# Routed adapters taken a whole layer of a pair at a time, and one rotation of eight PSUM banks, in a four-layer conditional residual kernel

## The chip, the core and the metric

The kernel runs on one core of one Trainium2 chip. The metric is the device time of one execution in microseconds (us); smaller is better. A core has a matrix engine (PE), which reads a stationary and a moving operand from the on-chip memory SBUF and writes sums into PSUM, two engines for elementwise work (DVE and ACT), a third that here does the convolution's additions and the gathers (POOL), and a queue engine (SP) that issues most of the transfers from device memory.

## What is computed

`x` has 32 batch rows of 64 x 1024 numbers. Four residual layers follow each other; `itok_...` are integers for each row.

```python
x = x + L0(x, ..., length=itok_B_78_3631)      # a long convolution along the 1024 axis, masked by length
x = x + einsum('bsi,boi->bso', x, W1[itok_B_0_15])   # one of 16 matrices of 1024 x 1024 for each row
x = x + einsum('bij,bkj->bik', x, W2[itok_B_1_14])   # the same with a second set
x = x + L3(x, ..., lora_indices=itok_B_2_6)    # gate, up and down projections (1024 to 2752 to 1024)
                                               # with a rank-16 correction chosen for each row
```

All of it is in 32-bit floats. The second and third layers are called adapters here: each batch row needs its own 4 MB matrix, used for only 64 rows of `x`.

## The kernel before

**Chunks.** The 32 batch rows are cut into four chunks of eight (`NCK`, `BC`). The convolution is done first for all chunks. Then the adapters of chunk 0 run alone. After that, `ffn(c, ...)` (line 446) runs the fourth layer of chunk c, and between its steps it does the adapters of chunk c+1. Chunk 3 has nothing to mix in.

**An adapter.** `adapter(w, layer, b0, pending)` (line 159) takes one of the two layers for a pair of batch rows. Its loop over eight blocks `kt` of the contracted axis loads two tiles of 512 KB, one for each row of the pair (lines 184 to 187), and issues four matmuls of 64 columns by 512 (line 191). They add into two PSUM banks `acc`. Two ACT copies take the banks to `y` (line 201). `residual` (line 206) transposes `y` back through eight PE transposes into two banks `py` and adds them to `x` on DVE (line 214); it runs inside the adapter that follows. A chunk has four pairs and two layers, so eight adapters, and `adapters` (line 216) chains them.

**Pieces.** `adapter` is a generator. Before, it yields after the fourth `kt` and at its end, so each adapter is two pieces with eight tiles each, and a chunk has `NPIECE` = 16 pieces. The closure `other` (line 453) adds up shares of the fourth layer's steps: 4 for each gated step (line 464) and 5 for each down step (line 556), 113 in a chunk. It takes the next piece whenever `due[1] * 113 < due[0]`, where `due[0]` grows by the share times `NPIECE + 1`. The last piece of the chain is the residual of the last adapter.

**The fourth layer's steps.** `gated` (line 369) goes over 11 blocks `m` of the hidden axis, and for each over two halves g (gate and up). Such a step loads two 512 KB tiles `wf` (line 381), makes three combinations of them on DVE (`stationary`, lines 356 to 359: sums `s1`, `s2`, `s4`, and one difference that overwrites a tile), and issues seven products of four matmuls (lines 386 and 399 to 412). The first product reads a loaded tile as it is; the second reads `s2`, so it needs both tiles and two DVE operations. Three banks `pf` take the products. Ahead of each `m`, `expand` (line 320) puts the low-rank correction into four banks `pe`, which ACT copies to `lt` (line 338). The down projection (line 493 on) loads two tiles `wd` for each segment of three blocks and uses four banks `po` for each of four `h`.

**Buffers.** The tiles `wa`, `wf` and `wd` share one rotation of nine buffers (`wpool`, tag `w`): the load of a tile is issued on SP only when the tile nine places earlier has been read for the last time. PSUM has eight banks. Before, six of them rotate under the tag `ps` (`ps_tile`), and two under the tag `acc` (`acc_tile`), which only adapters use.

**Order.** PE's order is that of the program text (`manual_schedule`). The other engines' queues, SP's too, are ordered by a scheduler when the program is built, and each queue is then executed in order.

Of the kernel before, what the change touches and what calls it, by code (L numbers as in the profile page):

```python
# [8 lines left out]
F32 = mybir.dt.float32  # L9
# [7 lines left out]
P = 128  # L17
# [4 lines left out]
BC = B // NCK  # L22
# [9 lines left out]
KH = KT // 2  # L32
R = 16
NE = 16
NPIECE = 2 * BC
AT_GATED, AT_DOWN = 4, 5
GROUPS = (8, 8, 16, 16, 16)
HG = max(GROUPS)
# [25 lines left out]
def kernel(  # L64
# [24 lines left out]
    xpool = ctx.enter_context(tc.tile_pool(name="xpool", bufs=2))  # L89
    wpool = ctx.enter_context(tc.tile_pool(name="wpool", bufs=9))  # L90
    psum = ctx.enter_context(
        tc.tile_pool(name="psum", bufs=6, space=bass.MemoryType.PSUM)
    )

    dpool = ctx.enter_context(
# [2 lines left out]

    def ps_tile(name):
        return psum.tile([P, 512], F32, tag="ps", name=name)  # L100


    def acc_tile(name):
        return psum.tile([P, 512], F32, tag="acc", name=name, bufs=2)

    cst = cpool.tile([P, CO_N], F32, tag="cst", name="cst")
    ident = cst[:, CO_ID : CO_ID + P]
# [51 lines left out]
    def adapter(w, layer, b0, pending):  # L159
        c, lo = b0 // BC, (b0 % BC) * H  # L160
        es = []
        for b in (b0, b0 + 1):
            with ExitStack() as after:
                if len(loads) > 1:

                    after.enter_context(tc.issue_after(loads[-2]))
                es.append(
                    nc.values_load(
                        ids_sb[0:1, layer * B + b : layer * B + b + 1],
                        engines=[SP],  # L170
                        min_val=0,
                        max_val=NE - 1,
                    )
                )
        acc = [acc_tile(f"pa{layer}_{b0}_{i}") for i in range(2)]
        for kt in range(KT):
            if kt == KH:
                yield
            if kt == (c == 0) and pending:
                residual(*pending.pop())  # L180
            wts = []
            for s, e in enumerate(es):
                name = f"wa{layer}_{b0 + s}_{kt}"
                wt = early.pop(0) if early else wpool.tile([P, L], F32, tag="w", name=name)
                load = nc.sync.dma_start(
                    wt, w[bass.ds(e, 1), kt].rearrange("e p f -> p (e f)")
                )
                wts.append(wt)
            for i in range(2):
                for s in range(2):  # L190
                    nc.tensor.matmul(  # L191
                        acc[i][s * H : (s + 1) * H, :],
                        xs[c][:, kt, lo + s * H : lo + (s + 1) * H],
                        wts[s][:, i * 512 : (i + 1) * 512],
                        start=(kt == 0),
                        stop=(kt == KT - 1),
                    )
        loads.append(load.ins)
        y = ypool.tile([P, L], F32, tag="y", name=f"y{layer}_{b0}")
        for i in range(2):  # L200
            copy = nc.scalar.copy(y[:, i * 512 : (i + 1) * 512], acc[i])
        copies.append(copy.ins)
        pending.append((c, lo, y, f"{layer}_{b0}"))
        yield

    def residual(c, lo, y, name):
        for q in range(0, KT, 4):
            ps = ps_tile(f"py{name}_{q}").rearrange("p (k t) -> p k t", t=P)
            for i in range(4):
                nc.tensor.transpose(  # L210
                    ps[:, i, :], y[:, (q + i) * P : (q + i + 1) * P], ident
                )
            cols = xs[c][:, q : q + 4, lo : lo + P]
            nc.vector.tensor_add(cols, ps, cols)  # L214

    def adapters(c):

        pending = []  # L220
        n = BC // 2
        for i in range(n + 1):
            if i < n:
                yield from adapter(w1, 0, c * BC + 2 * i, pending)
            if i > 0:
                yield from adapter(w2, 1, c * BC + 2 * i - 2, pending)
        residual(*pending.pop())
# [218 lines left out]
    def ffn(c, xb, others):  # L446
# [6 lines left out]
        def other(share, of=2 * FM * AT_GATED + (2 * KH - 3) * AT_DOWN):  # L453
            due[0] += share * (NPIECE + 1)
            while due[1] * of < due[0]:
                next(others, None)
                due[1] += 1
# [509 lines left out]
```

## Time and profile before

| what | value |
|---|---|
| time, median of three runs | 2477.97 us (2476.69 to 2479.43) |
| profiled execution: its time, and its span | 2475.95 us, 2474.2 us |
| PE busy | 2393.5 us, 97% of the span |
| DVE, ACT, POOL busy | 45%, 14%, 5% |
| DMA, mean over the span | 202 GB/s |

The span is the time from the first to the last instruction of one profiled execution. The kernel has these stages in it: convolution to about 209 us, the adapters of chunk 0 to 373 us, the start of the fourth layer to 395 us, the fourth layer of chunks 0, 1 and 2 with adapters between its steps to 2050 us, and that of chunk 3 alone to the end.

A line of a group reads: source line, engine, operation, output and inputs by name, shapes, count, then busy time, the mean duration of one in ns, and the idle time of the engine just before them with what ended it. A 32-bit matmul of the program shows as two records. A line of the waits reads: who waited for whom, the total in us, how many times, and the longest one.

### The profile page before, as it was taken

The page shows a single profiled execution, that of the slowest core. Times are in us where ns is not written, and L with a number is a line of the kernel's source. Part 1 is how long each engine was busy: PE and PEld are TensorE (multiplying, and loading weights), DVE is VectorE, ACT ScalarE, POOL GpSimd, SP SyncE. Part 2 cuts the span into 40 slices and gives each one's busy share as a digit, 9 for nine tenths or more (in the row PEclk, how much of TensorE's full clock was granted, in tenths as well). Part 3 has the DMA queues.
Part 4 walks back from the last instruction along what each step waited for, and adds up shares of the span by engine and source line. Part 5 has one row for each costly group of instructions (what it writes and reads, how often), then busy time and mean ns, then how long its engine had stood idle before and what let it go on. Part 6 is the DMA issues. An engine that isn't in the chain of part 4 may idle for free.

```text
span 2474.2 us, 35037 instructions
## 1 busy us (share of the span) xinstructions
PE 2393.5 (97%) x13600; PEld 1804.0 (73%) x13600; DVE 1116.5 (45%) x2127; ACT 344.5 (14%) x656; POOL 130.8 (5%) x136
## 2 busy tenths in 40 slices
PE   3899998999999999999999999999999999999999
PEld 3895335777777787777777687777777688888887
DVE  9611003444344554444345454445345546554554
ACT  4100001111011111111011111111011102110110
POOL 3431000000000000000000000000000000000000
PEclk9999999999999999999999999999999999999999
DMA  6789997656566547655665547555655543223221
GB/s 247 253 290 356 409 409 268 246 183 225 174 225 229 183 125 261 225 204 197 203 217 212 175 139 268 213 200 203 210 206 204 181 152 117 88 69 109 94 63 62
DMA packets 176184, 500.54 MB, mean 202 GB/s; under 512 B 19794, under 2 KB 69266, under 8 KB 174994
## 3 DMA queue, kind: packets, MB, share of 16 engines
q1 hardware_dynamic: 146338, 461.82, 52.8%
q10 hardware_dynamic: 25584, 22.85, 2.8%
q0 software_dynamic: 4096, 13.63, 1.7%
q8 instruction: 107, 1.75, 0.3%
q14 instruction: 59, 0.48, 0.1%
HBM read 485.36 MB, written 12.88 MB: 201 GB/s over the span
## 4 chain that ended last, share of the span: by engine, by line
PE 88%; DMA 8%; DVE 4%; issue 0%; ACTq 0%; SPq 0%; POOL 0%; ACT 0%; DVEq 0%
PE pf L386 42%; PE po L515 22%; PE pa L191 14%; DMA wa<-in_w 5%; PE pc L804 5%; PE pe L328 2%; PE py L210 1%; PE pl_d L285 1%; DMA xd<-x 1%; PE po L311 1%; DMA x<-xd 1%; DMA out_y<-x 0%; DVE bk L620 0%; DVE bsp L614 0%; DMA wf<-in_wu 0%; PE pl_u L285 0%
## 5 line engine op out<-in xcount | busy, mean ns | idle before, releaser
L386 PE MATMUL pf<-xd,wf 128*128 128x256 f32 (+1 forms) x2816 | 670.0, 382 | 8.9 <-ACT lt L338 8.9
L386 PEld LDWEIGHTS pf<-xd,wf 128*128 128x128 f32 (+1 forms) x2816 | 523.8, 188 | 108.2 <-issue 9.7
L386 PE MATMUL pf<-xd,s 128*128 128x256 f32 (+1 forms) x2112 | 500.5, 380 | 0.3 <-DVE s L357 0.3
L191 PE MATMUL pa<-wa,x 128*64 128x512 f32 x2032 | 482.9, 598 | 12.4 <-DMA wa<-in_w 8.5
L386 PEld LDWEIGHTS pf<-xd,s 128*128 128x128 f32 (+1 forms) x2112 | 396.6, 188 | 61.9 <-issue 0.7
L191 PEld LDWEIGHTS pa<-wa,x 128*64 128x64 f32 x2032 | 147.8, 136 | 312.6 <-issue 248.6
L515 PE MATMUL po<-act,wd 128*128 128x256 f32 x704 | 177.0, 385 | 0.0
L804 PE MATMUL pc<-uf,hk 128*128 128x256 f32 (+7 forms) x1024 | 154.3, 315 | 21.1 <-DMA hk<-kp 11.9
L515 PE MATMUL po<-actd,s 128*128 128x256 f32 x704 | 173.0, 379 | 0.1
L515 PE MATMUL po<-actd,wd 128*128 128x256 f32 x704 | 172.9, 379 | 0.0
L804 PEld LDWEIGHTS pc<-uf,hk 128*128 128x128 f32 x1024 | 149.9, 197 | 25.4 <-issue 15.2
L411 DVE TENSOR_TENSOR c<-pf,u 128x256 f32<-128x256 f32 (+1 forms) x88 | 37.3, 424 | 266.5 <-PE pf L386 266.5
L515 PEld LDWEIGHTS po<-act,wd 128*128 128x128 f32 x704 | 130.3, 190 | 31.5 <-issue 8.3
L515 PEld LDWEIGHTS po<-actd,s 128*128 128x128 f32 x704 | 133.5, 190 | 18.9 <-DVE s L357 0.6
L515 PEld LDWEIGHTS po<-actd,wd 128*128 128x128 f32 x704 | 133.6, 190 | 18.4
L234 POOL DMA_INDIRECT bgu<-in_bgu,rows x44 | 46.9, 1066 | 1809.3 <-PE pe L328 1690.8
L338 ACT COPY lt<-pe 128x512 f32<-128x512 f32 (+1 forms) x176 | 90.4, 598 | 277.9 <-PE pe L328 142.1
L356 DVE TENSOR_TENSOR s<-wf 128x512 f32<-128x512 f32 x88 | 60.7, 690 | 128.9 <-DMA wf<-in_wu 56.1
L415 DVE TENSOR_TENSOR c<-c,lt 128x1024 f32<-128x1024 f32 (+1 forms) x88 | 107.5, 1222 | 5.1 <-DVE c L413 0.5
L214 DVE TENSOR_TENSOR x<-py,x 128x512 f32<-128x512 f32 x64 | 42.9, 688 | 144.1 <-PE py L210 143.9
L356 DVE TENSOR_TENSOR s<-wd 128x384 f32<-128x384 f32 x64 | 33.4, 522 | 141.5 <-PE po L515 96.7
L409 ACT COPY c<-pf 128x256 f32<-128x256 f32 (+1 forms) x88 | 32.8, 372 | 417.4 <-PE pf L386 417.4
(148 smaller groups left out, 1671.2 us busy)
## 6 DMA issues: line engine op xcount, KB each, us to landing
wa<-in_w SPq DMA_DIRECT2D x508, 512.0 KB, 7.0
wf<-in_wg SPq DMA_DIRECT2D x88, 512.0 KB, 4.0
wf<-in_wu SPq DMA_DIRECT2D x88, 512.0 KB, 4.3
wd<-in_wd SPq DMA_DIRECT2D x96, 384.0 KB, 4.1
hk<-kp SPq DMA_DIRECT2D x32, 1024.0 KB, 7.6
x<-in_xt SPq DMA_DIRECT2D x4, 2048.0 KB, 13.4
uf<-in_xf SPq DMA_DIRECT2D x16, 512.0 KB, 7.7
wd<-in_wd SPq DMA_DIRECT2D x32, 256.0 KB, 3.1
```

The costliest lines, as they stand in the source:

```text
L191: nc.tensor.matmul(acc[i][s * H : (s + 1) * H, :], xs[c][:, kt, lo + s * H : lo + (s + 1) * H], wts[s][:, i * 512 : (i + 1) * 512], start= ...
L214: nc.vector.tensor_add(cols, ps, cols)
L234: nc.gpsimd.indirect_dma_start(out=t, out_offset=None, in_=table, in_offset=bass.IndirectOffsetOnAxis(ap=rows[:, c, piece : piece + 1], axis=0
L328: nc.tensor.matmul(ps[:n, at_ : at_ + 2 * H], bt[pair(j), g, i, :n], tms["gu"[g]][pair(j)], start=(g + i == 0), stop=True, skip_group_chec ...
L338: nc.scalar.copy(lt[:n, :, 2 * H * j : 2 * H * (j + 1)], ps[:n].rearrange("p (i t) -> p i t", i=4),)
L356: nc.vector.tensor_add(s1, a21, a22)
L386: nc.tensor.matmul(ps, ws[j][:, kt, :n], xb[j][:, kt, :], start=start and kt == 0, stop=kt == KH - 1, skip_group_check=True,)
L409: nc.scalar.copy(cq[:n, 0], pa)
L411: nc.vector.tensor_add(cq[:n, 1], pb, u[:n])
L415: nc.vector.tensor_add(cf, cf, lt[:n, g].rearrange("p i t -> p (i t)"))
L515: nc.tensor.matmul(pss[j], ws[j][:k, i, :], ab[m - m0][j], start=(m == m0 and home[j] % 2 == 0), stop=(m == m1 - 1), skip_group_check=True,)
L804: nc.tensor.matmul(ps[:, j, d * B :], hk[:, j, d * P : (d + 1) * P], uf[:, i + j, : KT - d, :].rearrange("p k b -> p (k b)"), start=(d == ...
```

## The change

An adapter is no longer split: the yield after the fourth `kt` goes, so that a piece is a whole layer of a pair, with 16 tiles and 32 matmuls, and a chunk has `NPIECE` = 8 pieces. The two tags of PSUM become one: adapters' sums are taken with `ps_tile` from one rotation of eight banks, together with all other users.

```diff
-NPIECE = 2 * BC
+NPIECE = BC
...
-        tc.tile_pool(name="psum", bufs=6, space=bass.MemoryType.PSUM)
+        tc.tile_pool(name="psum", bufs=8, space=bass.MemoryType.PSUM)
...
-    def acc_tile(name):
-        return psum.tile([P, 512], F32, tag="acc", name=name, bufs=2)
...
-        acc = [acc_tile(f"pa{layer}_{b0}_{i}") for i in range(2)]
+        acc = [ps_tile(f"pa{layer}_{b0}_{i}") for i in range(2)]
         for kt in range(KT):
-            if kt == KH:
-                yield
             if kt == (c == 0) and pending:
                 residual(*pending.pop())
```

## The prediction

> **What bounds the kernel now.** I read the page's busy line first, then PE's waits, then busy time by stage, and last the timelines around one piece.
>
> ```profile
> span 2474.2 us, 35037 instructions
> PE 2393.5 (97%) x13600; PEld 1804.0 (73%) x13600; DVE 1116.5 (45%) x2127; ACT 344.5 (14%) x656; POOL 130.8 (5%) x136
> ```
>
> PE is the bound, and 80.7 us of the span are idle. PE's waits after 396 us, when the fourth layer runs, are nearly nothing:
>
> ```profile
> PE pf L386 <- ACT lt L338: 8.9, 1, 8.9
> PE pa L191 <- DMA x<-xd: 3.2, 2, 1.9
> PE pf L386 <- DVE s L357: 0.3, 1, 0.3
> ```
>
> The first is one stall at 386.5 to 395.4; the others are 3.5 us in 1650. So the change has almost nothing to win where it acts, and every new PE stall there lengthens the run by its own length. Busy time by stage (length; busy time of PE, PEld, DVE, ACT, POOL; granted clock, DMA share, GB/s):
>
> ```profile
> 209.00:373.00 164.00, 153.19 (x572) 48.80 (x572) 10.65 (x17) 12.16 (x19) 5.32 (x6) 1.00 1.01 399
> 396.00:950.00 554.00, 553.85 (x3120) 412.63 (x3119) 253.42 (x472) 81.72 (x158) 13.10 (x12) 0.99 0.58 200
> ...
> 410.00:424.00 14.00, 14.00 (x66) 9.71 (x63) 5.09 (x8) 2.27 (x5) 0.00 (x0) 1.00 0.82 312
> 462.00:476.00 14.00, 14.00 (x94) 9.31 (x91) 6.80 (x13) 2.70 (x6) 0.95 (x1) 1.00 0.84 320
> ```
>
> The adapters of chunk 0 (first row) run against a full DMA: 399 GB/s, and the page shows slices of 409. A tile of 512 KB then takes 524288 / 409000 = 1.28 us. Mixed into the fourth layer, DMA is at 58% on average, but a piece's loads come in a burst (last two rows: 312 and 320 GB/s with the burst's slow start, 1.66 us a tile). PE's and DVE's timelines around two pieces:
>
> ```profile
> 426.73 7.09 PE L191 MATMUL pa<-wa,x 128*64 128x512 f32 x32
> 433.75 0.73 PE L328 MATMUL pe<-tm_g,bgu 32*128 32x128 f32 x16
> 436.68 1.89 PE L386 MATMUL pf<-xd,s 128*128 128x256 f32 x8
> ...
> 433.83 0.69 DVE L356 TENSOR_TENSOR s<-wf 128x512 f32<-128x512 f32 x1 [2.21 <-DMA wf<-in_wg]
> 434.56 0.69 DVE L357 TENSOR_TENSOR s<-s,wf 128x512 f32<-128x512 f32 x1
> ...
> 487.90 0.69 DVE L356 TENSOR_TENSOR s<-wf 128x512 f32<-128x512 f32 x1 [3.19 <-DMA wf<-in_wu]
> 488.63 0.69 DVE L357 TENSOR_TENSOR s<-s,wf 128x512 f32<-128x512 f32 x1
> ...
> 489.47 1.97 PE L386 MATMUL pf<-xd,s 128*128 128x256 f32 x8
> ```
>
> A piece of eight tiles takes PE 7.02 us (the chain of waits steps by 7.02), 0.88 us a tile, which is faster than DMA can bring one. What saves it is the rotation of nine. Behind the first piece the next step's `s2` is ready at 435.25 and used at 436.68: 1.43 us to spare, 1.1 of them lent by `pe`. Behind the second it is ready at 489.32 and used at 489.47: nothing to spare. The half pieces already sit at the edge.
>
> **What the Trainium skill says.** "DMA: Bandwidth & Descriptors", section "Where 436 GB/s comes from", puts the ceiling of the DMA engines at 435 GB/s; the trace's 409 agrees in kind, and says no deeper queue makes a burst faster than about 1.28 us a tile. Its section "Queues, rings and completion order" says that each engine serves its rings in turn and that completions needn't come in order; the trace shows loads of a burst landing 3.4 to 8.9 us after their issue. "TensorE: Matmul & The Clock Gate", section "What's actually happening", says that an idle window of about 3.4 us halves the clock; here the clock is 0.50 from 391.4 to 401.6, which starts 4.9 us into the stall. "PSUM — Partial Sum Buffer", specifications, gives eight banks; six and two already used all, so none is gained, only shared.
>
> **The change part by part.** No matmul, copy or load is added or removed; what follows is order and waits. Sums are against the profiled execution, 2475.95 us, which is 2.0 below the median of 2477.97.
>
> *Eight banks in one rotation.* Waits of PE on PSUM were one, the 8.9 us. In the built program's order the third product of the first gated step no longer waits for ACT, as it gets a fresh bank. But the fourth product reuses the second's bank, which ACT copies at line 402 only after the same late `lt` copies (from 394.75, behind transfers on ACT's queue); it started at 399.1 and will again. So the third product (1.76 us) runs at 386.5, and PE then idles to 399.05. The half clock now ends 6.2 us after that restart instead of after 395.4: 3.65 us later, with one product done ahead, 1.9 us lost. Bounds: -12.0 (the stall and 3.1 us of half clock go, if ACT's copies come early) to +3.1 (all of a second slow stretch). I take +1.9. Elsewhere an adapter draws four banks from the rotation, and the eighth bank back was emptied steps ago: nothing. In chunk 0's adapters PE no longer waits 0.7 us for ACT at each boundary, but DMA is full there: nothing.
>
> *Whole adapters in the fourth layer.* There are 3 chunks x 8 = 24, instead of 48 halves. By the shares they come after gated steps 0, 3, 6, 9, 13 and 16 and down steps 0 and 2: three inside an `m` (plain), three ahead of a `pe` of 1.1 us (covered), two ahead of a `wd` segment. SP's order is now 16 `wa`, then the next step's two `wf`.
>
> Work through a plain one, with t = 0 at its first matmul. Seven tiles are there, as before; the eighth's buffer comes free two products earlier. Tile 9 goes out at -1.0, when the last product of the step ahead is done (`py` takes 1.09 between). Each later tile waits for the tile nine before: tiles 10 and 11 for the first two, at 1.76; 12 and 13 at 3.5; 14 and 15 at 5.3; 16 at 7.0, `wf0` at 7.7 by SP's spacing of 0.6, `wf1` at 8.9. A lone load lands 3.45 us after issue (the minimum was 3.4), so tile 10 at 5.3 and each next one r later. With r = 1.28: tile 16 at 13.0 (PE wants it at 12.3), `wf1` at 15.5, `s2` 1.5 later at 17.0, while PE wants it at 14.04 + 1.76 = 15.8. Stall 1.2 us. With r = 1.4: 2.2; covered 1.4, `wd` (0.75 of the bytes, DVE operations of 0.52) 1.6. That is the low route, since it gives a lone load's latency to tile 10.
>
> The high route starts from the margins seen: eight more tiles take 8r on DMA and 7.02 on PE. At r = 1.4 they lose 4.2 us, against a margin of 0 (plain) or 1.43 (covered): stalls of 4.2 and 2.8; for `wd` 2.8 too.
>
> | | low, r = 1.28 | high, r = 1.4 | taken |
> |---|---|---|---|
> | plain, 9 of them | 1.2 | 4.2 | 2.7 |
> | covered, 9 | 0.7 | 2.8 | 1.8 |
> | ahead of `wd`, 6 | 0.7 | 2.8 | 1.7 |
> | sum | 21 | 80 | 51 |
>
> I take the middle: a longer burst reaches full rate, but its start is slow. Stalls of 1 to 3 us should not halve the clock, as the 1.9 us wait for `x` at 956 us didn't.
>
> *What is queued behind.* DVE is in order. After an adapter it has the step's four combinations, then the next step's four, then the step's evictions; the next step's `wf` land some 2.6 us later, and the evictions are due 5 us after the first product, so I cost this at nothing. SP's loads behind the burst are for steps 12.3 us apart. ACT's `y` copies stand at the adapter's end in both. The last residual moves from gated step 21 to step 20: nothing.
>
> Sum: 2475.95 + 51 + 1.9 = 2529; against the median 2530.
>
> **The rivals.**
> - *In-order queues add to it.* If `wf` of the next step come so late that evictions behind their combinations are late too, PE waits for a bank in the middle of a step. For: in the new DVE order combinations for two steps ahead stand before the fifth eviction. Against: about 5 us of room. At 2 us for each of 24: 2530 + 48 = 2578.
> - *The nine buffers still cover it.* Should tiles land as fast as PE reads, only the clock's 1.9 is left: 2480. For: average DMA use is 58%. Against: 0.88 us a tile is under the 1.28 seen at full rate, and the margin is 0 to 1.4.
> - *Faster.* One mechanism: the banks. If at 386.5 the fresh bank lets PE go on, 12.0 us are won: 2466, with the bursts covered. It decides if ACT's copy of the second product ends before 388.3 instead of at 399.05. Against: that copy stands behind the same `lt` copies in ACT's order.
>
> **How the numbers follow.** Forecast 0.74, queues 0.13, covered 0.08, faster 0.05. The forecast's own range is 2475.95 + 21 + 0 to 2475.95 + 80 + 3.1, plus 2 for the median: 2499 to 2561. That holds little more than 0.7, so the range reaches into the queues' case and a little below: 2490 to 2580. A measurement of this kernel tells 0.2% (5 us) from no change; slower by more takes the forecast and the queues, 0.87, same 0.08, faster 0.05.
>
> **What would show it.** PE's waits after 396 us should show `pa` on DMA `wa` and `pf` or `po` on DVE `s`, in 24 places, about 50 us in sum, with the plain adapters worst; adapters take more than 14.04 us from the sixth `kt` on. At 386 us: one product, then a wait for ACT to 399. DMA at about 400 GB/s in the bursts. Wrong would be PE waits under 10 us in all there, or waits of `pf` on evictions.

## The result, and the profile after

The changed kernel takes 2542.07 us (median of 4 runs, 2538.7 to 2543.91) against 2478.12 us for the kernel before on the same chip: a ratio of 1.0257, 95% interval 1.0239 to 1.0274. The forecast was 2530; it comes out 64 us slower where 52 were forecast. The profiled execution took 2542.59 us. Two lines of its page:

```profile
span 2540.8 us, 35003 instructions
PE 2441.1 (96%) x13600; PEld 1816.5 (71%) x13600; DVE 1104.9 (43%) x2127; ACT 341.4 (13%) x656; POOL 131.1 (5%) x136
```

PE issues the same 13600 records, and is busy 47.6 us longer with them, while its idle time grows from 80.7 to 99.7 us. Read alone, the busy line says that PE has become slower. PE's waits from 396 us on:

```profile
PE pa L185 <- DMA wa<-in_w: 12.3, 51, 1.6
PE pf L380 <- ACT c L396: 6.4, 1, 6.4
PE pa L185 <- DMA x<-xd: 3.2, 2, 1.7
PE pf L380 <- DVE s L351: 2.2, 9, 0.3
```

Adapters now wait for their tiles, 51 times, which never happened in this stage before; the nine waits for `s` are the nine adapters with a gated step right behind them. All four sum to 24 us, though, while this stage has grown by 60. PE's timeline of the first adapter in the fourth layer (start, length, instructions in a row; in brackets the idle time ahead) shows where the rest hides:

```profile
413.33 9.66 PE L185 MATMUL pa<-wa,x 128*64 128x512 f32 x42
423.23 4.43 PE L185 MATMUL pa<-wa,x 128*64 128x512 f32 x14 [0.24 <-DMA wa<-in_w]
427.82 1.07 PE L185 MATMUL pa<-wa,x 128*64 128x512 f32 x2 [0.17 <-DMA wa<-in_w]
429.10 1.93 PE L185 MATMUL pa<-wa,x 128*64 128x512 f32 x6 [0.21 <-DMA wa<-in_w]
430.96 1.99 PE L380 MATMUL pf<-xd,wf 128*128 128x256 f32 x8
433.21 1.97 PE L380 MATMUL pf<-xd,s 128*128 128x256 f32 x8 [0.25 <-DVE s L351]
```

The first 42 records, five of the eight `kt` blocks and a little more, take 0.23 us each; the last 22 take 7.73 us, 0.35 each, with only 0.38 us of it shown as idle. The group of these matmuls over the three chunks (output and inputs, count, then busy time, mean of one in ns, idle time ahead) in the kernel before and after:

```profile
L191 PE MATMUL pa<-wa,x 128*64 128x512 f32 x1536 | 340.2, 595 | 3.2 <-DMA x<-xd 3.2
```

```profile
L185 PE MATMUL pa<-wa,x 128*64 128x512 f32 x1536 | 385.8, 600 | 15.8 <-DMA wa<-in_w 12.3 <-DMA x<-xd 3.2
```

The mean of one hardly moves (595 to 600 ns), yet their common busy time grows by 45.6 us: fewer of them lie on top of each other. The single records show how. Where nothing is late, they start in twos 7 ns apart, each 592 ns long, and a new two starts every 0.43 us. At the first late tile of this adapter two records start singly, at 421.96 and 422.39 us, and the next two only at 423.23. A single one counts as "busy" just as two at once do, so that only 0.24 us are shown as idle. I take the twos to be the two rows of the pair, of which one has its tile and the other waits; the records don't name the row. So waiting shows as idle time in part only, 12.3 us over all adapters; the length of an adapter shows all of it. Measured from its first matmul to the next product, an adapter takes 16.53 us on the mean of the 24 (15.77 to 17.64).

What DMA and SP do about the first adapter: busy time by stage as in the prediction, and SP's issues (start, length of the row of issues).

```profile
396.00:970.00 574.00, 562.84 (x3064) 410.92 (x3062) 247.22 (x467) 79.26 (x154) 11.84 (x11) 0.99 0.53 190
415.00:431.00 16.00, 15.30 (x59) 4.26 (x55) 1.42 (x2) 2.63 (x3) 0.00 (x0) 1.00 0.93 364
...
414.00:422.00 8.00, 8.00 (x39) 2.62 (x36) 2.42 (x2) 2.34 (x2) 0.00 (x0) 1.00 0.74 276
422.00:431.00 9.00, 8.30 (x27) 1.93 (x24) 0.00 (x0) 0.59 (x1) 0.00 (x0) 1.00 1.03 415
```

```profile
409.98 10.80 SPq L179 DMA_DIRECT2D wa<-in_w  x9
420.90 1.60 SPq L375 DMA_DIRECT2D wf<-in_wu  x2
```

DMA is at 53% over the stage and at 93% within the adapter: 276 GB/s up to 422 us, then 415. The clock stays at full speed. The eighth tile goes out at 409.98, the ninth at 413.43, and the sixteenth at 420.44 as the last of this row of nine, 7.11 us after the first matmul, where the prediction had 7.0; the two `wf` come after. Counted over all 24 adapters, blocks 0 to 4 take 1.72 to 1.77 us, which is PE's own pace, block 5 2.17, block 6 2.57 and block 7 3.15. 2.57 is two tiles of 1.28 us: there PE runs at the rate of DMA. (Block 7 is counted up to the next product, which without any wait makes it 1.82 instead of 1.72.)

Where the 66.6 us between the two profiled executions lie: 60.3 between the start of the fourth layer of chunk 0 and that of chunk 3 (1635.2 to 1695.5 us), and 6.3 before it. Of the latter, 3.0 are a later start of the adapters of chunk 0 (213.6 against 210.6 us) and 3.3 their longer time (166.6 against 163.3 us). I don't put them down to the change: in the runs below, kernels with the old banks start these adapters at 211.5 to 213.5 us and take 163.3 to 166.8 us for them.

### The profile page after: what moved, and what is told of

Same layout as the page of the kernel before. It is cut to its first block, busy times and chain, and to the rows that moved or that the text cites. A ratio compares the mean times of both kernels' runs of the same rounds, so it can differ in the third digit from the quotient of the medians.

```text
span 2540.8 us, 35003 instructions
## 1 busy us (share of the span) xinstructions
PE 2441.1 (96%) x13600; PEld 1816.5 (71%) x13600; DVE 1104.9 (43%) x2127; ACT 341.4 (13%) x656; POOL 131.1 (5%) x136
## 4 chain that ended last, share of the span: by engine, by line
PE 81%; DMA 15%; DVE 4%; issue 0%; ACT 0%; SPq 0%; POOL 0%; ACTq 0%; DVEq 0%
PE pf L380 41%; PE po L509 21%; DMA wa<-in_w 10%; PE pa L185 10%; PE pc L798 4%; DMA wf<-in_wu 3%; PE pe L322 2%; PE py L204 1%; PE pl_d L279 1%; PE po L305 1%; DMA x<-xd 1%; DMA out_y<-x 0%; DVE bk L614 0%; DMA raw_d<-in_ad 0%; DVE s L350 0%
## 5 line engine op out<-in xcount | busy, mean ns | idle before, releaser
L185 PE MATMUL pa<-wa,x 128*64 128x512 f32 x2032 | 526.4, 601 | 28.7 <-DMA wa<-in_w 24.0
L185 PEld LDWEIGHTS pa<-wa,x 128*64 128x64 f32 x2032 | 158.1, 136 | 375.4 <-issue 223.9
L195 ACT COPY y<-pa 128x512 f32<-128x512 f32 x64 | 37.4, 585 | 583.6 <-PE pa L185 583.6
```

The lines of the kernel that those rows point to most:

```text
L185: nc.tensor.matmul(acc[i][s * H : (s + 1) * H, :], xs[c][:, kt, lo + s * H : lo + (s + 1) * H], wts[s][:, i * 512 : (i + 1) * 512], start= ...
```

## The experiments

The theory under test: a piece of 16 tiles outlasts the nine buffers, and from the sixth block on PE waits for the transfer of tiles. The rivals: the banks do it, or DVE's and SP's order does.

**One part each.** Whole adapters with six and two banks as before (first edit), and eight banks with halves as before (second).

```diff
-NPIECE = 2 * BC
+NPIECE = BC
...
-            if kt == KH:
-                yield
```

```diff
-        tc.tile_pool(name="psum", bufs=6, space=bass.MemoryType.PSUM)
+        tc.tile_pool(name="psum", bufs=8, space=bass.MemoryType.PSUM)
...
-        acc = [acc_tile(f"pa{layer}_{b0}_{i}") for i in range(2)]
+        acc = [ps_tile(f"pa{layer}_{b0}_{i}") for i in range(2)]
```

> Whole pieces alone, PSUM as before (six banks and two). Transfers theory (a burst of 16 tiles outruns nine buffers; each late tile costs 1.28 us): the full loss without the banks' part, 2534 to 2542 us, adapters of the fourth layer 2.3 to 2.7 us longer than 14.04 us each. Banks theory (the shared rotation makes PE wait): back near 2478 us.

> Eight banks in one rotation alone, half pieces as before. Transfers theory: 2476 to 2484 us; the third product of the first gated step no longer waits for ACT, the fourth waits instead, and a second slow stretch of the clock costs about 2 us. Banks theory: most of the loss, over 2510 us. If the shared rotation freed PE, under 2472 us.

The first took 2535.1 us against 2477.71, a ratio of 1.0227 (1.0211 to 1.0243). Its group of adapter matmuls:

```profile
L189 PE MATMUL pa<-wa,x 128*64 128x512 f32 x1536 | 384.7, 599 | 18.0 <-DMA wa<-in_w 13.5 <-DMA x<-xd 4.1
```

The same stall, without the new banks: its 24 adapters lose 63.7 us against unstalled ones (next experiment), 63.5 in the changed kernel. The second took 2482.29, a ratio of 1.0017 (1.001 to 1.0023): 4.2 us of cost, 2.5 to 5.7 by the interval. Of PE's waits up to 420 us it shows the one that the prediction gave to the banks:

```profile
PE pf L382 <- ACT c L398: 8.5, 1, 8.5
```

So the pieces make the loss, and the banks a few us. The one profile of the second has the fourth layer of chunks 0 to 2 only 1.7 us longer than before (1636.9 against 1635.2), but its execution of 2478.43 us is among the fastest of that kernel's 21, so it can't place the rest.

**The tiles themselves.** If the transfer sets the pace, half the tiles must cure it with the pieces as long as they are. From the changed kernel:

```diff
-            wts = []
-            for s, e in enumerate(es):
+            share = c > 0 and kt % 2
+            wts = wts if share else []
+            for s, e in enumerate(() if share else es):
```

> The changed kernel, but in chunks 1 to 3 an adapter loads tiles only for every second block and uses each for two blocks, so half of these adapters' contracted rows meet the wrong weights: same matmuls, half the transfers. Transfers theory: 2474 to 2486 us, PE waits on wa and s after 396 us near zero. Queues theory (in-order DVE and ACT delay PE after a long piece): stays over 2515 us.

It took 2473.76 us, 0.9983 (0.9976 to 0.999) of the kernel before. PE in the first adapter:

```profile
413.44 13.95 PE L186 MATMUL pa<-wa,x 128*64 128x512 f32 x64
```

All 64 records stand in one row: no waits for `wa`, none for `s`. To the next product each of its 24 adapters takes 13.88 or 13.89 us. Against that length those of the changed kernel lose 2.65 us where a gated step follows, 2.48 ahead of `pe` and 2.89 ahead of `wd`; in sum 63.5. The second product after the nine plain ones comes another 0.41 us late: 3.7. Together 67.2, and the stage is 66.5 us shorter than in the changed kernel (1629.0 against 1695.5). The order of PE and DVE with its long pieces costs nothing by itself. SP issues half as many loads here too, so this run alone doesn't part the issuing from the transfer; the trace of the changed kernel does, as there the sixteenth tile goes out when the prediction had it, at 7.11 us, and lands late (the times of landing are in the section on the prediction). The stage is 6.2 us shorter than in the kernel before as well; 3.6 of these come from the joint (two halves take 2 x 7.02 us, a whole 13.88), and the other 2.6 lie in the products between the adapters, for a reason I can't name.

**One buffer less.** `bufs=8` for `wpool`, in the changed kernel and in the kernel before.

> The changed kernel with eight load buffers instead of nine. Transfers theory: one tile more has to come inside each of 24 adapters, at the 1.28 us of a full queue: 24 x 1.28 = 31 us more than the changed kernel, 2568 to 2580 us. If late tiles were only a matter of landing order or latency, one buffer less costs under 10 us.

> The kernel before (half pieces, six banks and two) with eight load buffers instead of nine. If half pieces sit at the edge of what nine buffers cover (spare time of 0 to 3 us behind each of 48 pieces, one tile 1.04 to 1.28 us): the tight ones begin to stall, 0.2 to 0.8 us a piece in the mean, 2486 to 2516 us. If nine buffers had room to spare for halves: within 3 us of before.

With whole adapters 2566.93 us, 1.0354 (1.0338 to 1.037): 25 us more than the changed kernel, 1.04 for each of 24. The adapters' lengths alone give 1.12 (90.3 us lost instead of 63.5). That is below the expected 2568, and a buffer is worth somewhat less than a tile's 1.28 us. With halves 2491.37, 1.0048 (1.0032 to 1.0063), 12.5 us more than the kernel before on its chip. PE's waits from 420 us:

```profile
PE pf L386 <- DVE s L357: 8.2, 11, 1.6
```

The halves wait only behind the piece, for the next step's `s` (and 1.0 us for its `wf`), as "at the edge" in the prediction said; the wholes wait within.

**Shorter pieces.** If length is the cost, quarters of four tiles should be free or better. From the kernel before, with `NPIECE = 4 * BC`:

```diff
-            if kt == KH:
+            if kt and kt % 2 == 0:
                 yield
```

> The kernel before with an adapter in four pieces of two blocks (NPIECE of 32, a yield before blocks 2, 4 and 6). Transfers alone: its stalls were 0.3 us, so nothing is left to win, 2476 to 2478 us. If each join of two pieces saves PE about 0.16 us, as adapters that wait for nothing show (13.95 us whole against twice 7.09 us less the overlap), 48 more breaks cost 48 x 0.16 = 7.5 us: 2483 to 2488 us.

Neither: 2523.37 us, 1.0171 (1.0157 to 1.0185). PE's waits from 420 us, and PE's and DVE's timelines around one of the longest:

```profile
PE pf L386 <- DVE c L407: 24.1, 26, 3.1
```

```profile
511.63 1.89 PE L386 MATMUL pf<-xd,wf 128*128 128x256 f32 x8
516.08 3.43 PE L386 MATMUL pf<-xd,s 128*128 128x256 f32 x8 [2.56 <-DVE c L407]
...
512.53 0.69 DVE L356 TENSOR_TENSOR s<-wf 128x512 f32<-128x512 f32 x1 [7.00 <-DMA wf<-in_wu]
513.14 0.42 DVE L403 TENSOR_TENSOR u<-c,u 128x256 f32<-128x256 f32 x1
513.47 0.68 DVE L357 TENSOR_TENSOR s<-s,wf 128x512 f32<-128x512 f32 x1
514.07 0.42 DVE L405 TENSOR_TENSOR c<-pf,u 128x256 f32<-128x256 f32 x1
514.41 0.68 DVE L358 TENSOR_TENSOR wf<-wf,wf 128x512 f32<-128x512 f32 x1
515.01 0.68 DVE L359 TENSOR_TENSOR s<-wf,s 128x512 f32<-128x512 f32 x1
515.61 0.41 DVE L407 TENSOR_TENSOR c<-pf,c 128x256 f32<-128x256 f32 x1
```

No adapter of this stage waits for a tile. But the built order of DVE now has the next step's combinations (lines 356 to 359) ahead of and between the present step's evictions (403 to 407), and DVE waits 7.00 us for a tile that PE doesn't need yet; PE's sixth product waits for the bank that line 407 empties. This is the rival of the in-order queues, which the changed kernel doesn't show. The waits are about half of the 44.5 us lost. By the lengths in the profile, the stage has grown by 46.9 us (1682.1 against 1635.2), 39.7 of them in the fourth layer's products and 5.0 in the pieces of adapters; about a third of the loss I can't tie to one wait. Cutting the work finer moved the stall from the buffers into an order; it doesn't say that longer pieces are better.

**A better version.** The stall of the kernel before at 386 us is ACT: its queue issues the loads of the `at_d` columns (in `columns`), the fourth and fifth of them at 384.86 and 391.16, each right after a write of `xd` has landed (384.39, 391.14), and the copies `lt`, which empty the banks, stand behind them at 394.75. I moved the call of `columns` behind the first gated step of each block, and bound its issue to ACT's copy of line 409 in the first half of that step (`marks[-2]`). In a second version eight banks in halves come on top, and in a third the mark is that of the step's second half (`marks[-1]`).

```diff
-            at = columns(ad[:, block, :, : 2 * nm], c, 2 * nm, f"d{block}_{c}")
             acts = []
             for m in range(m0, m1):
                 acts.append(gated(c, m, xb, between))
+                if m == m0:
+                    with tc.issue_after(marks[-2]):
+                        at = columns(ad[:, block, :, : 2 * nm], c, 2 * nm, f"d{block}_{c}")
```

> The kernel before, with the low-rank columns of the down projection loaded and copied on ACT's queue only after the first gated step of their block, so that ACT's copies of PSUM at the start of the fourth layer are not queued behind them. If the stall of 8.9 us at 386 us and its 3.1 us of half clock are due to that order: 2464 to 2469 us. If the same stall only moves to the next transfer that the busy DMA delays (parked x, wf, wa): 2472 to 2479 us.

> Half pieces, the down projection's columns after the first gated step of their block, and the eight banks in one rotation. If the shared rotation costs only through the moved stall at the start of the fourth layer, that stall is gone here and the time is that of the same kernel with six banks and two, 2468 to 2473 us. If it costs in the convolution or the adapters of chunk 0 or elsewhere, the 4 to 5 us remain: 2474 to 2477 us.

> The kernel before with the columns' loads on ACT's queue only after the second gated step of their block. The 1.9 us wait for ACT's copy that was left with the first step goes: 2466 to 2470 us. If PE then waits for these columns at the down projection's low-rank product: over 2471 us.

The first took 2470.6 us, 0.9964 (0.9951 to 0.9978), faster than both kernels, though 1.6 us above what was expected. PE at the start of the fourth layer:

```profile
388.08 3.04 PE L386 MATMUL pf<-xd,wf 128*128 128x256 f32 x8
390.96 1.89 PE L386 MATMUL pf<-xd,s 128*128 128x256 f32 x8
392.69 1.89 PE L386 MATMUL pf<-xd,wf 128*128 128x256 f32 x8
394.41 1.89 PE L386 MATMUL pf<-xd,s 128*128 128x256 f32 x8
...
415.90 1.99 PE L386 MATMUL pf<-xd,s 128*128 128x256 f32 x8 [1.86 <-ACT c L402]
```

The stall of 8.9 us and the half clock behind it are gone, and a wait of 1.86 us is left in the step that now has the loads. (The 3.04 us of the first line are another stretch of half clock, 386.8 to 390.2.) With eight banks as well it took 2472.18, 0.9979 (0.9971 to 0.9988). By its time it lies in the first range, that of a cost at the start of the fourth layer alone; by its ratio it is 0.0015 of 2478 or 3.7 us worse than with the old banks, and the two intervals just overlap. So the run doesn't settle where the banks cost their 4.2 us. In the one profile of each, the fourth layer of chunks 0 to 2 takes 5.9 us longer with eight banks (1632.1 against 1626.2), at the wait for `x` at 956 us and at three waits for `s`, not at its start; whether the banks cause these is not shown.

The third, one gated half later, took 2512.54, 1.0133 (1.0118 to 1.0149). The chain of waits at one place (start, length, what):

```profile
426.88 6.13 DMA wa<-in_w
433.01 0.02 issue
433.03 0.09 ACT at_d L264
433.11 0.16 issue
433.27 0.02 ACTq L402
433.29 1.12 issue
434.40 1.06 ACT y L201 x2
435.47 0.50 ACT lt L338
435.97 0.04 issue
436.01 1.22 PE pf L386 x2
```

ACT's copy `at_d` now stands ahead of the adapter's `y` copies and of `lt`, and waits for its loads with them behind it: eight waits of `pf` for `lt`, 27.9 us from 380 us on. The kernel before has 8.9 us of this wait, in one place. I had expected a gain, from the load's place alone; the copy that belongs to it is what costs.

## Why the prediction was right or wrong

- **"Every new PE stall there lengthens the run by its own length"**: right. 67.2 us of stalls in the trace, 66.5 us between the runs with and without them.
- **Pieces, sum 51**: right in kind, too small. The plain adapters were taken at 2.7 and lost 3.06 (2.65 in them, 0.41 behind), the covered ones at 1.8 and lost 2.48, those ahead of `wd` at 1.7 and lost 2.89. The sum came to 67.2, less 3.6 for the joint that the prediction didn't count. The 51 was the middle between a low route that gave 21 and a high one that gave 80. The reason given for it, that the start of a burst is slow, is borne out (276 GB/s, then 415), but nothing gave its size; that the middle came within a quarter of the measured sum is in part luck.
- **The step that failed** is the cover. The low route had the sixteenth tile 0.7 us late, but put the stall at `wf1` and `s2` (wanted at 15.8), and both routes let `pe` or the smaller `wd` hide part. In the trace the adapter's own sixteenth tile is late first and by more: its last matmuls can't start, and nothing that stands behind the adapter hides that. This is why the three kinds lose nearly the same.
- **"Tile 10 at 5.3 and each next one r later"**: the start was right, the next tiles were slower. The trace tells some of the times of landing, counted from the first matmul: tile 10 at 5.40 to 5.46 us (four adapters), tile 13 at 10.0 to 10.9 (five), where r = 1.28 gives 9.1, tile 15 at 12.8 to 13.7 (six) for 11.7, and the second load behind the tiles at 16.7 to 17.1 (four) for 15.5. So tiles 11 to 13 came about 1.66 us apart, while DMA was not yet full, and the loads behind them about 1.29 apart, at the rate that the low route had. By the lengths of the adapters, tile 16 lands some 14.6 us after the first matmul, not at 13.0. That lag of 1.3 to 1.6 us I had not priced in the low route; why DMA isn't full in the first 8 us of a burst stays open. A lone load (3.4 us from issue to landing) takes some 2.1 us beside its 1.28 of transfer. "DMA: Bandwidth & Descriptors" of the Trainium skill, section "Anatomy of one DMA — SWDGE (gpsimd) path", gives a fixed cost of about 2.0 us for transfers that POOL issues; these are SP's, and agree.
- **"PE's waits ... about 50 us in sum"**: the places were right (51 waits for `wa`, nine for `s`, from the sixth block on), the sum wasn't. As waits the profile shows 14.5 us, not far above the 10 that were to count against the forecast; the loss is in the lengths. "DMA at about 400 GB/s in the bursts" holds for their second half.
- **Banks, +1.9**: right in the mechanism, to the product. The third product runs and the fourth waits for ACT:

```profile
393.18 2.74 PE L380 MATMUL pf<-xd,s 128*128 128x256 f32 x8
395.75 1.89 PE L380 MATMUL pf<-xd,wf 128*128 128x256 f32 x8
404.00 3.78 PE L380 MATMUL pf<-xd,s 128*128 128x256 f32 x8 [6.36 <-ACT c L396]
```

  The last line's 3.78 us are the half clock after the stall (401.7 to 408.5); the 2.74 of the first line are an earlier stretch of it (388.1 to 394.9). The size, in the kernel with nothing but the banks, was 4.2 us (2.5 to 5.7), of which the upper bound of +3.1 holds only the low end.
- **"Stalls of 1 to 3 us should not halve the clock"**: it held here, 0.99 over 574 us with waits of at most 1.7 us, but not as a rule. "TensorE: Matmul & The Clock Gate" of the Trainium skill, section "What's actually happening", names an idle window of about 3.4 us; the 6.36 us wait is over it and was followed by half clock. The other traces have shorter waits that were followed by it for 3.41 us: 2.28 us with eight banks in halves, 2.10 and 2.56 in the quarters, and 1.69 ahead of the first adapter of this kernel (213.6 us). The same 1.69 us in the kernel before was not, and a wait of 2.30 us with whole adapters and the old banks was not. Within each profile the stretches of half clock start a whole number of times 3.41 us apart, whatever stands between, so where a wait falls on that grid seems to count beside its length; no run here varies it by design.
- **The queues' rival (2578)**: didn't happen here, PE never waits for an eviction on DVE. It is real in the quarters.
- **Covered (2480)**: didn't happen. Tiles land slower than PE reads them, as said.
- **Faster (2466)**: didn't happen. ACT's copy of the second product came late, as said. The moved columns win part of what was to be had there, 0.36%.

## What to carry to other kernels

A kernel at 58% of its DMA can still be short of DMA within a burst: ask how many tiles one piece eats at PE's pace, and how many the rotation holds; beyond that a tile costs, as a first estimate, its transfer less its compute, 1.28 less 0.88 us here. For the seven tiles beyond nine that is 2.8 us, and 2.65 were measured inside the adapters next to a gated step; but one buffer taken away cost 1.04 to 1.12 us, not 0.40, so the estimate doesn't carry far. Look first for the tile of the piece itself that comes last, since nothing that stands behind the piece can hide it. And when an edit moves a load, look at what is queued behind both the load and the operation that reads it, on the engines that serve the critical one.

## What was not expected of the hardware

- The wait of one of two matmuls that run at the same time hardly shows as idle time: 12.3 us of waits for `wa` against 63.5 us of longer adapters.
- Loads of 512 KB in the queue of a long piece land late though DMA is at its full rate: the `wf` of chunks 0 to 2 whose landing the trace tells took 7.9 to 11.0 us from issue to landing (16 loads of 132), and at most 6.4 us in the kernel before (87 of 132).
- A wait of PE of 1.69 us was followed by half clock in the changed kernel, and the same wait in the kernel before was not.
